# Storing a finished row tile one step later: a GpSimd-issued DMA in a two-layer attention and feed-forward kernel

## The chip, the cores and the metric

The kernel runs on one core of a Trainium2 chip. The time is that of the device in microseconds (us), of one launch. A core has the engines PE (TensorE, matmuls; PEld are its weight loads), DVE (VectorE), ACT (ScalarE), POOL (GpSimd) and SP (SyncE). In this kernel DMAs are issued from SP's queue and from POOL's queue, and run on the core's 16 DMA engines.

## The reference

All arrays are float32. `x` has 2 sequences of 2048 rows of 1024.

```python
x = x + attention(layernorm(x))        # one head: Wqkv to 3 x 256, softmax, Wo back to 1024
n = layernorm(x)
h      = relu(n @ up_w) ** 2           # 1024 -> 2048
shared = h @ down_w                    # 2048 -> 1024
lat    = (n @ fc1_w) @ expert_w        # 1024 -> 512 -> 512
routed = (lat * top2_sum(n @ gate_w)) @ fc2_w      # 512 -> 1024
x = x + layernorm(shared + routed) * ln_gamma + ln_beta
```

The change lies at the end of the last line: the layer norm of a finished tile, and its store to the result.

## The kernel before, in words

Each float32 operand is split into a high part, which ACT casts, and a low part, which DVE makes by a subtraction; a product is then three matmuls (line 130: high by high, low by high, high by low). All 4096 rows are handled in 8 row blocks of 512, and a row block in 4 row tiles of 128.

The attention comes first and is not touched by the change. Then comes the feed-forward part, a loop over `b` = 0 to 3. One `b` takes two row blocks (r = 0 and 1) together, so that a scheme of seven products (`p1` to `p7`) stands in for the eight block products of a two by two split. A `b` has two stages:

- The **up stage** runs over 70 chunks, `m` = 0 to 69, one weight piece each, 12 matmuls per chunk (`pu`).
- The **down stage** runs over the products in the order p1, p2, p6, p5, p3, p7, p4 (`j` = 0 to 6), 10 chunks each (`k` = 0 to 9), also 12 matmuls per chunk (`pd`). The rows of the first block (r = 0) are complete after p3, those of the second (r = 1) after p4. The results lie in 4 buffers `y` of the pool `unit` (14 buffers for `y`, `h`, `xh`, `xl` and `res`), two row tiles in each.

The weight pieces go round a ring of 7 buffers `w`. `stage` (L786) issues a load on SP's queue: either a raw piece `w<-wt` (L798), or one that was already split, `w<-w_p` (L795). A raw piece is cast by ACT (L815), its low half made by DVE (L823), and in b=0 for every other piece, in b=1 for every raw piece, the split piece is written back to memory from POOL's queue (`w_p<-w`, L826) to be loaded again later. The left operands of the down stage, `sp`, are cast by ACT (L1052) and finished by DVE (L1057).

A finished tile of `y` then goes through the steps of the class `Out`. `out_step` keeps a list of tiles for each step, and a call moves each tile one step further:

1. the residual row is loaded from `x1` on SP's queue (L960);
2. `add_beta`: the row vector beta is added to it by an accumulating DMA on POOL's queue (L963), and `first`: ACT sums y (L259);
3. `second`: ACT sums the squares (L271, L272);
4. `write`: DVE makes the reciprocal and two passes over y (L276, L976, L977), and POOL's queue issues the store (L978).

`out_step` is called every second chunk: in the up stage at odd `m` below 15 (tiles of r = 1 of the `b` before), in the down stage at even `k` of p7 and at k = 0 and 2 of p4 (tiles of r = 0). The last four tiles of the program take a path of their own (`late`), tile by tile behind the last matmuls.

The order is written by hand: the part lies under `tc.manual_schedule()`, so each engine and each queue runs its instructions in the order in which the program issues them, and waits at the head of its queue until that instruction's inputs are there.

Of the kernel before, what the change touches and what calls it, by code (L numbers as in the profile page):

```python
# [25 lines left out]
def kernel(  # L26
# [923 lines left out]
    class Out:  # L950
# [22 lines left out]
        def write(self):  # L973
            y, rs = self.y, self.m.inverse()
            stt = nc.vector.scalar_tensor_tensor
            stt(y, y, self.m.nm, gamma_sb, ALU.add, ALU.mult)  # L976
            stt(y, y, rs, self.res, ALU.mult, ALU.add)  # L977
            nc.gpsimd.dma_start(out=of[ds(self.n * W + self.t * P, P), :], in_=y)  # L978

    res_pair, todo, loaded, first, second = [], [], [], [], []

    def out_step():

        if second:
            second.pop(0).write()
        if first:
            second.append(first.pop(0))
            second[-1].second()  # L990
        if loaded:
            first.append(loaded.pop(0))
            first[-1].add_beta()
            first[-1].first()
        if todo:
            loaded.append(Out(*todo.pop(0)))
# [11 lines left out]
    with tc.manual_schedule():  # L1008
        for b in range(NBB):
# [70 lines left out]
            for m, (p, i) in enumerate(UP):  # L1080
                flush()
                w = next_piece()
                if p != "p2":
                    acc[i] = Pass3(acc_bank("pu"), NCC // 2)
                ps = acc[i].ps
                if p == "p2":
                    acc[i].more()
                for c in range(NCC // 2):
                    acc[i].add(piece(w, c, P, slice(0, P)), piece(X[p], c, W, slice(0, W)))
                lat, pair = i >= HU // P, i % 2 and i < HU // P  # L1090
                c22, c21 = h_at("22", i), h_at("21", i) if m >= 2 * NK else None
                if p == "p1":
                    nc.scalar.copy(c22, ps)
                elif p == "p2":
                    if lat:
                        add(h_at("11", i), ps, rwb[0], ALU.mult)
                    else:
                        relu(h_at("11", i), ps)
                        if pair:
                            square(h_at("11", i, 2))  # L1100
                elif p == "p4":
                    nc.scalar.copy(c21, ps)
                elif p == "p6":
                    add(c22, ps, c22, ALU.subtract)
                    add(c21, c21, c22, ALU.subtract)
                elif p == "p5":
                    add(c22, c22, ps, ALU.add)
                elif p == "p3":
                    c12 = h_at("12", i)
                    add(c12, c22, ps, ALU.add)  # L1110
                    if lat:
                        add(c12, c12, rwb[0], ALU.mult)
                    elif pair:
                        relu(h_at("12", i, 2), h_at("12", i, 2))
                        square(h_at("12", i, 2))
                else:
                    add(c21, c21, ps, ALU.add)
                    add(c22, c22, ps, ALU.subtract)
                    if lat:
                        add(c21, c21, rwb[1], ALU.mult)  # L1120
                        add(c22, c22, rwb[1], ALU.mult)
                    elif pair:
                        for v in ("21", "22"):
                            relu(h_at(v, i, 2), h_at(v, i, 2))
                            square(h_at(v, i, 2))

                if m % 2 and m < 15:
                    out_step()
                if b == 0 and m in (0, 1, 2, 4, 6, 8, 9, 10, 11, 12, 13):
                    norm2.step()  # L1130

                m4 = 12 if b == 0 else 10
                if m == m4:
                    x_t[1] = norm2.x
                    X["p4"] = new_x()
                if m > m4 and (m - m4) % 2 and (m - m4) // 2 < NB:
                    split_x(x_t[1], 1, (m - m4) // 2, X["p4"], split_late)
                elif m >= 2 * NK and p != "p7":
                    n = {"p4": "p6", "p6": "p5", "p5": "p3", "p3": "p7"}[p]
                    if i == 1:  # L1140
                        X[n] = new_x()
                    if i % 2 and i < 2 * NB:
                        if p == "p4":
                            sums_x(x_t, i // 2)
                        r_, f_ = PLACE[n]
                        split_x(x_t[r_], f_, i // 2, X[n], split_late)

                if m == 0:
                    ga = half("ga")[: 2 * NE, :]
                    nc.scalar.copy(ga, gate_part(X["p1"], 0))  # L1150
                elif m == 2:
                    gs = half("gs")[: 2 * NE, :]
                    add(gs, ga, gate_part(X["p2"], 1), ALU.add)
                    gt = Gate(gs)
                elif (p, i) == ("p4", 1):
                    add(ga, ga, gate_part(X["p4"], 1), ALU.add)
                elif (p, i) == ("p7", 0):
                    add(ga, ga, gate_part(X["p7"], 0), ALU.subtract)
                    gt = Gate(ga)
                if m == 6 or (p, i) == ("p7", 3):  # L1160
                    gt.largest()
                elif m == 10 or (p, i) == ("p7", 6):
                    rwb[p == "p7"] = gt.spread()
                if p == "p7" and i >= NK - 5:
                    step_s()
# [16 lines left out]
            for j, p in enumerate(("p1", "p2", "p6", "p5", "p3", "p7", "p4")):  # L1182
# [12 lines left out]
                for k in range(NK - late):  # L1195
                    flush()
                    w, s = next_piece(), next_s()
                    for t in range(NB):
                        down(t, s, w)
                    if more:  # L1200

                        if j < 6 and k < NK - 2:
                            (norm1, norm2)[j // 3].half_step()
                        if j >= 5 and k % 2 and k < 2 * NB:
                            n = "p1" if j == 5 else "p2"
                            if k == 1:
                                X[n] = new_x()
                            split_x(norm1.x, j - 5, k // 2, X[n], split_late)
                    if not more and j == 2 and k == 0:
                        ended(1)  # L1210
                        tiles = todo[-NB:]
                        del todo[-NB:]
                    elif not more and j == 3 and k % 2 == 0 and k < 2 * NB:
                        tiles[k // 2] = Out(*tiles[k // 2], row("res"))
                    elif not more and j == 4 and k % 2 == 0 and k < 2 * LATE:
                        load_early(k // 2)
                        if k < 2 * NB:
                            tiles[k // 2].add_beta()
                    if j == 5 and k % 2 == 0 or j == 6 and k in (0, 2):
                        out_step()  # L1220
                if late:
                    last_w = [next_piece() for _ in range(late)]
# [5 lines left out]
                for t in range(NB):  # L1228
                    for s, w in last if late else ():
                        down(t, s, w)  # L1230
                    ps, u, v = accs[t].ps, y_at(1, 0, t), y_at(1, 1, t)
                    if p == "p1":
                        nc.scalar.copy(u, ps)
                    elif p == "p2":
                        nc.scalar.copy(y_at(0, 0, t), ps)
                    elif p == "p6":
                        add(u, ps, u, ALU.subtract)
                    elif p == "p5":
                        add(v, u, ps, ALU.add)
                    elif p == "p3":  # L1240
                        add(y_at(0, 1, t), u, ps, ALU.add)
                    elif p == "p7":
                        add(v, v, ps, ALU.subtract)
                    else:
                        add(u, ps, u, ALU.subtract)
                    if late:
                        tiles[t].first()
                        tiles[t].second()
                        if t:
                            tiles[t - 1].write()  # L1250
                if late:
                    tiles[-1].write()
                if p == "p3":
                    ended(0)
                elif p == "p4" and not late:
                    ended(1)
            if more:
                t1 = norm1.x
        while todo or loaded or first or second:
            out_step()  # L1260


# [41 lines left out]
```

## Time and profile before

| | |
|---|---|
| median of 3 runs | 2384.47 us (2383.08 to 2388.02) |
| the profiled execution | 2384.76 us, of which the span is 2382.9 |
| granted TensorE clock | 0.995 |
| PE busy | 2335.8 us, 98% |
| DVE, ACT, POOL busy | 61%, 47%, 13% |
| DMA | 603.99 MB, mean 253 GB/s over the span |
| stores of y (L978) | 32, of 512 KB, 539 ns of POOL each, 7.2 us to landing (2.8 to 13.0) |
| beta adds (L963) | 32, of 512 KB, 10.7 us to landing |
| write-backs (L826) | 140, of 512 KB, 4.8 us to landing |
| POOL waits at L978 for y | 182.8 us in all |
| DVE waits at L977 for beta | 22.1 us in all, 15 times |

A row of a timeline reads: start, duration, engine, line, operation, output and input, count, and in brackets how long the engine was idle ahead of it and what ended that. A row of waits reads: engine, line, what it waited for, and the sum, the number and the longest of those waits. The span is what the profiler sees of one execution; the time beside it holds 1.9 us more around it. "Landing" is the time from the issue of a DMA to the arrival of its data.

### The profile page before, as it was taken

The numbers are of one execution on the slowest core, as the hardware profiler recorded it, in microseconds if no ns is written. First come the engines' busy times: TensorE is split into PE (matmuls) and PEld (weight loads), VectorE is DVE, ScalarE is ACT, GpSimd is POOL, SyncE is SP. The second block draws the span as 40 slices with busy tenths as digits, with TensorE's granted clock in tenths as the row PEclk, the third lists the DMA queues.
The fourth block names the chain that finished last, engine by engine and source line by source line (L and its number), as shares of the span: only waits on it lengthen the run. The fifth ranks groups of instructions, "written<-read, shape, count | busy, mean of one in ns | idle before, by whom it ended". The sixth has DMA issues, their size and how long they took to land.

```text
span 2382.9 us, 29281 instructions
## 1 busy us (share of the span) xinstructions
PE 2335.8 (98%) x10704; PEld 1921.8 (81%) x10704; DVE 1461.4 (61%) x2168; ACT 1131.4 (47%) x1846; POOL 298.1 (13%) x450
## 2 busy tenths in 40 slices
PE   8999999999998999999999999999999999999998
PEld 7888878888886778788778888878888877888886
DVE  5566459888877466697746467644446563445545
ACT  6555455555444543676552374644145454214224
POOL 3222111012110010011210011210000010000001
PEclk9999999999999999999999999999999999999999
DMA  5977884999996666787997789997557798655695
GB/s 196 318 257 269 278 204 127 298 315 319 290 239 181 219 228 185 228 271 259 336 309 241 237 283 333 319 342 241 193 194 262 264 330 283 208 192 184 202 312 191
DMA packets 225807, 603.99 MB, mean 253 GB/s; under 512 B 18768, under 2 KB 80720, under 8 KB 223616
## 3 DMA queue, kind: packets, MB, share of 16 engines
q1 hardware_dynamic: 152160, 334.02, 41.2%
q0 software_dynamic: 73504, 268.11, 36.8%
q8 instruction: 85, 1.39, 0.2%
q14 instruction: 58, 0.48, 0.1%
HBM read 448.96 MB, written 210.76 MB: 277 GB/s over the span
## 4 chain that ended last, share of the span: by engine, by line
PE 88%; issue 5%; DMA 4%; DVE 1%; ACT 1%; POOL 1%; SPq 0%; POOLq 0%; DVEq 0%; ACTq 0%
PE pu L130 29%; PE pd L130 26%; PE ps L130 7%; PE pq L130 7%; PE po L130 7%; PE pv L130 4%; PE pw L130 3%; DMA w<-wt 1%; PE pg L872 1%; PE pf L130 1%; DMA xt<-xt_d 1%; DMA w<-w_p 1%; PE psum L619 1%; DMA res<-in_L_ffn_ln_beta_dram 0%; DMA ew<-in_L_ffn_expert_w_dram 0%
## 5 line engine op out<-in xcount | busy, mean ns | idle before, releaser
L130 PE MATMUL pd<-w,sp 128*128 128x512 f32 x3336 | 762.5, 390 | 11.0 <-DVE sp L1057 5.6
L130 PEld LDWEIGHTS pd<-w,sp 128*128 128x128 f32 x3336 | 626.5, 188 | 145.8 <-DVE sp L1057 8.4
L130 PE MATMUL pu<-xh,w 128*128 128x512 f32 x2240 | 694.4, 391 | 7.2 <-ACT w L815 5.1
L130 PEld LDWEIGHTS pu<-xh,w 128*128 128x128 f32 x2240 | 419.6, 188 | 99.0 <-ACT w L815 6.1
L130 PE MATMUL pu<-xl,w 128*128 128x512 f32 x1120 | 436.2, 389 | 0.0
L130 PEld LDWEIGHTS pu<-xl,w 128*128 128x128 f32 x1120 | 210.4, 188 | 44.1 <-DVE xl L150 0.4
L1052 ACT CAST sp<-h 128x512 fp32r<-128x512 f32 x238 | 145.9, 618 | 193.1 <-PE pd L130 160.7
L1057 DVE TENSOR_TENSOR sp<-h,sp 128x512 fp32r<-128x512 f32 x238 | 162.4, 687 | 100.9 <-ACT sp L1052 100.6
L815 ACT CAST w<-w 128x512 fp32r<-128x512 f32 x210 | 128.3, 617 | 178.4 <-DMA w<-wt 144.7
L130 PE MATMUL po<-p,v 128*128 128x512 f32 x768 | 197.0, 395 | 2.6 <-ACT p L142 2.4
L823 DVE TENSOR_TENSOR w<-w 128x512 fp32r<-128x512 f32 x210 | 143.1, 686 | 91.3 <-ACT w L815 84.8
L130 PE MATMUL ps<-q,k 128*128 128x512 f32 x768 | 195.9, 393 | 1.8 <-DVE max L562 1.8
L130 PEld LDWEIGHTS ps<-q,k 128*128 128x128 f32 x768 | 142.4, 188 | 36.1 <-DVE max L562 6.8
L130 PEld LDWEIGHTS po<-p,v 128*128 128x128 f32 x768 | 144.1, 190 | 33.6 <-ACT p L142 3.2
L1002 ACT ACTIVATE h<-h 128x1024 f32<-128x1024 f32 x48 | 50.7, 1055 | 208.7 <-DVE h L1110 159.7
L826 POOL DMA_DIRECT2D w_p<-w x140 | 75.1, 537 | 583.1 <-DVE w L823 532.3
L150 DVE TENSOR_TENSOR xl<-xt,xh 128x512 fp32r<-128x512 f32 x104 | 71.6, 688 | 122.8 <-ACT xh L149 120.8
L557 ACT COPY s<-ps 128x512 f32<-128x512 f32 x128 | 74.8, 585 | 148.2 <-PE ps L130 147.7
L213 DVE STREAM_TRANSPOSE xblk<-xrow 128x1024 f32<-128x1024 f32 x60 | 121.1, 2019 | 9.6 <-ACT xrow L283 9.6
L562 DVE TENSOR_TENSOR max<-ps,max 128x512 f32<-128x512 f32 x120 | 82.3, 685 | 44.4 <-ACT s L557 44.1
L130 PE MATMUL pq<-xha,w_h 128*128 128x512 f32 x256 | 99.7, 389 | 0.0
L130 PE MATMUL pq<-xha,w_l 128*128 128x512 f32 x256 | 99.7, 389 | 0.0
(181 smaller groups left out, 3034.3 us busy)
## 6 DMA issues: line engine op xcount, KB each, us to landing
w<-w_p SPq DMA_DIRECT2D x350, 512.0 KB, 4.2
w_p<-w POOLq DMA_DIRECT2D x140, 512.0 KB, 4.8
w<-wt SPq DMA_DIRECT2D x210, 256.0 KB, 3.7
xt_d<-xblk POOLq DMA_DIRECT2D x56, 512.0 KB, 4.6
xt<-xt_d POOLq DMA_DIRECT2D x56, 512.0 KB, 6.6
wt<-in_L_ffn_up_w_dram POOLq DMA_DIRECT2D x9, 2048.0 KB, 25.1
wt<-in_L_ffn_down_w_dram POOLq DMA_DIRECT2D x9, 2048.0 KB, 32.3
xres<-in_L_attn_x_dram SPq DMA_DIRECT2D x32, 512.0 KB, 13.0
```

The source lines that it names most:

```text
L130: nc.tensor.matmul(self.ps, lhsT=a, rhs=b, start=self.i == 0, stop=self.i == self.n - 1, skip_group_check=self.on,)
L150: late_ops.append(lambda: nc.vector.tensor_tensor(lo, t, f32(hi), ALU.subtract))
L213: nc.vector.transpose(b.rearrange("p (q k i) -> p q k i", q=P // SQ, i=SQ), r.rearrange("p (k i q) -> p q k i", k=NCC, i=SQ),)
L557: nc.scalar.copy(s["s"][k // 4][:, ts(k % 4, W)], pm)
L562: nc.vector.tensor_tensor(s["max"], pm, s["max"], ALU.max)
L619: nc.tensor.matmul(pt[:, t : t + 1], lhsT=s["sum"][:, ds(i * W + t * P, P)], rhs=ones, start=i == 0, stop=i == 1,)
L815: nc.scalar.copy(w[:, 0:W], f32(w)[:, W : 2 * W])
L823: nc.vector.tensor_tensor(w[:, W : 2 * W], v[:, W : 2 * W], v[:, 0:W], ALU.subtract)
L826: nc.gpsimd.dma_start(out=kept[key], in_=w.bitcast(FP))
L1002: nc.scalar.activation(o, v, AF.Relu)
L1052: nc.scalar.copy(t[:, 0:W], v)
L1057: add(t[:, W : 2 * W], v, f32(t)[:, 0:W], ALU.subtract)
```

## The change

The store becomes a step of its own, `store`, behind `write`. `out_step` first stores the tile that the call before has written, then goes on as before. Since a tile now takes one call more, `out_step` is called once more in each stage: at m = 15 of the up stage and at k = 4 of p4. In the last four tiles the store follows directly on the write, as before.

```diff
             stt(y, y, self.m.nm, gamma_sb, ALU.add, ALU.mult)
             stt(y, y, rs, self.res, ALU.mult, ALU.add)
+
+        def store(self):
+            y = self.y
             nc.gpsimd.dma_start(out=of[ds(self.n * W + self.t * P, P), :], in_=y)
...
-    res_pair, todo, loaded, first, second = [], [], [], [], []
+    res_pair, todo, loaded, first, second, written = [], [], [], [], [], []
 
     def out_step():
 
+        if written:
+            written.pop(0).store()
         if second:
-            second.pop(0).write()
+            written.append(second.pop(0))
+            written[-1].write()
         if first:
             second.append(first.pop(0))
             second[-1].second()
...
-                if m % 2 and m < 15:
+                if m % 2 and m < 17:
                     out_step()
...
-                    if j == 5 and k % 2 == 0 or j == 6 and k in (0, 2):
+                    if j == 5 and k % 2 == 0 or j == 6 and k in (0, 2, 4):
                         out_step()
...
                         if t:
                             tiles[t - 1].write()
+                            tiles[t - 1].store()
                 if late:
                     tiles[-1].write()
+                    tiles[-1].store()
...
-        while todo or loaded or first or second:
+        while todo or loaded or first or second or written:
             out_step()
```

So the order in POOL's queue changes. Where the program had (b=1, p7) the store of tile 0, the beta add of tile 2, a write-back, the store of tile 1, the beta add of tile 3, it now has the beta add of tile 2, a write-back, the store of tile 0, the beta add of tile 3, a write-back, the store of tile 1. The order on the other engines and on SP's queue is the same.

## The prediction

> **What bounds the kernel now.** I read the page's totals first, then the table of windows over the stages that contain the change, then the waits of PE and of the DMA queues in those stages, and last the timeline of the worst one. The totals say that TensorE decides:
>
> ```profile
> PE 2335.8 (98%) x10704; PEld 1921.8 (81%) x10704; DVE 1461.4 (61%) x2168; ACT 1131.4 (47%) x1846; POOL 298.1 (13%) x450
> ```
>
> Whatever the change does, it can win only idle time of PE and lose only by making more of it. The windows (stretch, length, busy time of PE, PEld, DVE, ACT and POOL, granted clock, DMA share, GB/s) show where PE idles among the stages that run `out_step`:
>
> ```profile
> 1113.00:1189.00 76.00, 71.99 (x314) 58.30 (x313) 58.39 (x88) 47.79 (x92) 17.35 (x28) 1.00 0.97 324
> 1189.00:1535.00 346.00, 346.00 (x1534) 282.77 (x1533) 209.00 (x331) 172.91 (x293) 50.23 (x87) 1.00 0.85 286
> 1535.00:1590.00 55.00, 49.95 (x214) 39.07 (x213) 31.72 (x46) 22.87 (x47) 8.46 (x14) 1.00 1.02 354
> 1900.00:1985.00 85.00, 83.03 (x360) 67.58 (x359) 47.78 (x68) 39.93 (x76) 11.88 (x17) 0.98 0.92 315
> 1985.00:2359.00 374.00, 374.00 (x1657) 306.68 (x1656) 173.71 (x269) 125.11 (x204) 14.01 (x19) 1.00 0.70 230
> ```
>
> The first, third and fourth are the ends of the down stages (p7, then p4) of blocks b=0, 1 and 2: PE idles 76.00-71.99 = 4.01, 55.00-49.95 = 5.05 and 85.00-83.03 = 1.97 us. The up stages behind them and the last block up to 2359 us have none. So everything that the change can win is 4.0+5.0+2.0 = 11.0 us, 0.46% of the span. In each of the three the DMA engines are at 0.92 to 1.02 of their time. In b=1 PE is held back piece by piece (first the waits of PE from 1535 to 1590 us, then one of SP's queue from 1505 to 1590: sum, times, longest):
>
> ```profile
> PE pd L130 <- DVE sp L1057: 3.3, 4, 1.5
> PE pd L130 <- ACT junk L271: 1.7, 1, 1.7
> ```
>
> ```profile
> SPq L795 <- DMA w_p<-w: 37.9, 10, 9.1
> ```
>
> The reader should see the ring: SP may load a weight piece only when the slot's earlier piece has been written back (`w_p<-w` landed); ACT casts what lands, DVE makes the low half, PE multiplies, POOL writes back. The timeline of b=1 shows POOL's queue and DVE in it:
>
> ```profile
> 1545.16 0.54 POOL L978 DMA_DIRECT2D out_dram<-y  x1 [8.57 <-DVE y L977]
> 1546.05 0.87 POOL L963 DMA_DIRECT2D res<-in_L_ffn_ln_beta_dram  x1 [0.35 <-issue]
> 1547.78 0.55 POOL L826 DMA_DIRECT2D w_p<-w  x1 [0.86 <-DVE w L823]
> 1555.26 0.54 POOL L978 DMA_DIRECT2D out_dram<-y  x1 [6.92 <-DVE y L977]
> 1555.79 0.91 POOL L963 DMA_DIRECT2D res<-in_L_ffn_ln_beta_dram  x1
> 1561.86 1.29 DVE L977 SCALAR_TENSOR_TENSOR y<-y,rs,res 128x1024 f32<-128x1024 f32 x1 [1.20 <-DMA res<-in_L_ffn_ln_beta_dram]
> 1563.07 0.69 DVE L823 TENSOR_TENSOR w<-w 128x512 fp32r<-128x512 f32 x1
> 1564.41 5.74 PE L130 MATMUL pd<-w,sp 128*128 128x512 f32 x24 [1.50 <-DVE sp L1057]
> 1567.80 1.29 DVE L977 SCALAR_TENSOR_TENSOR y<-y,rs,res 128x1024 f32<-128x1024 f32 x1 [0.98 <-DMA res<-in_L_ffn_ln_beta_dram]
> ```
>
> The store of tile 0 stands in POOL for y (8.57 us), and the beta add of tile 2 stands behind it: it goes out at 1546.05, and tile 2's last DVE operation waits 1.20 us for it at 1561.86. Behind that on DVE are the low halves of w and of sp, and PE waits 1.50 us for the latter.
>
> **The change part by part.** It adds and removes no operation: 32 stores of 512 KB before and after, 539 ns of POOL each, and the order of instructions on PE, DVE, ACT and SP is the same. The two new calls of `out_step` (up chunk 15, p4 chunk 4) find only a store to do. The last four tiles keep their order. For the other 28, the store now stands behind the beta add that followed it, where there is one, and in b=0 and 1 mostly behind a write-back too.
>
> *The wait that goes.* Waits of POOL for y sum to 182.8 us over 32 stores, but POOL is busy 13%, so they cost nothing themselves. What counts is what stood behind them. Write-backs did not suffer: at 1547.78 one goes out 0.30 us after its DVE operation (1546.79+0.69), at 1569.99 0.29 us after, and in b=0 (1155.45 after 1154.24+0.68) 0.53 us, about POOL's own issue; I take 0. Beta adds did: those of tiles 2 and 3 go out 4 to 7 us earlier (tile 2 then waits only for its residual row, tile 3 no longer for y of tile 1). The DVE waits for tiles 2 and 3 then vanish: b=1 1.20+0.98, b=0 0.79 (tile 3). Those of tiles 0 and 1 (2.91 us at 1543.58, 1.34 in b=0) stay, because no store stood ahead of them. Of these waits PE loses what ends in its own stalls: 1.20 of the 1.50 us at 1564.41, the whole 0.20 us at 1570.35 (behind the 0.98), and 0.61 us at 1173.09 (behind the 0.79). Sum: 1.20+0.20+0.61 = 2.0 us gained. The limits: 0, if the weight piece behind each is late anyway, and the 11.0 us of all stalls. In b=2 DVE waits 2.37 and 1.97 us for these betas, but PE's only stall there is a weight load issued at 1936.38 that takes 18 us, so I take 0 of it (limits 0 and 1.97).
>
> *The traffic.* A beta add is 512 KB, which at the 354 GB/s of the b=1 window is 1.5 us of the DMA engines. Two in b=0 and two in b=1 come earlier, and about one store of each block leaves the stretch in which PE stalls. Here a rule speaks against the change. The stretch 1520 to 1590 us reads
>
> ```profile
> GB/s 321 288 379 417 380 406 424 393 367 272 234 265 373 426 369 281 307 397 419 419 327 262 368 408 320 260 389 415 404 391 316 383 287 339 417 426 419 353 323 375
> q0 software_dynamic: 3407, 12.37, 52.5%
> q1 hardware_dynamic: 4109, 12.64, 49.0%
> ```
>
> POOL's queue (q0) and SP's (q1) move equal bytes. If only the bytes counted, a store put off beyond the last stall would free 1.5 us in each of two blocks, 3.0 us in all. The Trainium skill, "DMA: Bandwidth & Descriptors", section "Queues, rings and completion order", says that each DMA engine takes turns between the queues that have work. By it SP's loads get their half for as long as POOL's queue holds anything, and betas brought forward keep it full: 0 from a later store. I take 0, since 12.37 against 12.64 MB is what turns would give, and keep -3.0 in the range. The other end is that each of the four early betas delays a weight transfer by its full 1.5 us: +6.0. The same page's "Specifications" give 358 GB/s from HBM as the limit of one core; at 354 the stalls would be pure bandwidth and no order could win anything. Slices of up to 426 GB/s in this same stretch say that it isn't a hard limit here, so I keep the 2.0.
>
> *The later release of y.* A chunk lasts 2.72 us (the spacing of SP's loads at 1520.08 and 1522.80). The last store of a first-half tile is now at p4 chunk 4, and the buffers of the tiles are claimed again from up chunk 2: 8 chunks, 21.8 us. Of a second-half tile it is up chunk 15, claimed six chunks on: 16.3 us. Stores land in 7.2 us, at most 13.0. Cover remains, so 0; if it were gone it would cost the excess of the landing over 16.3 us, and 13.0 is the longest seen. SP's order is unchanged and its loads wait for no store.
>
> Sum: -2.0 us. The profiled execution took 2384.76 us (its span 2382.9 and 1.9 around it), 0.3 above the median of 2384.47, so the difference is put on the median: 2382.5.
>
> **The rivals.** A measurement of this kernel tells about 0.2%, 4.8 us, from no change; the runs before spread over 4.9.
>
> *The ring loosens.* With the betas out of the way and the stores behind the write-backs in POOL's queue, each write-back lands sooner (it took 6.1 us from 1547.78, 7.6 from 1556.35), SP's 37.9+27.6 us of waiting in b=1 and b=0 shrink, and with them most stalls of both blocks: two thirds of 4.0+5.0, and 1 of b=2, is -7.0 us: 2377.5. For it: the ring is what PE waits for. Against: the first stalls (1548.14, 1552.44) come from transfers sent before the first store, and the DMA engines are full.
>
> *Early betas take the weights' place.* In b=1 the beta of tile 2 would go out near 1541 us, ahead of the write-back of 1547.78 and while the loads of 1533.68 and 1539.12 take 12 and 15 us to land. If all four early betas go on that path at 1.5 us each, and they then land no earlier for DVE, the time is 2384.5+5.9 = 2390.4. It decides when the write-back behind such a beta lands over 1.5 us later than the 6 to 7.6 us of now. Against: the loads' delay is already made by transfers sent before 1537.
>
> *Nothing moves.* [...]in b=2 and 3 no write-back lies between, and a store behind a beta that is ready goes out when y is done, as before. If the betas of b=0 and 1 were not what PE waits for, the time stays at 2384.5.
>
> **How the numbers follow.** The 2.0 us gain 0.40; nothing moves 0.10; the ring loosens 0.30; early betas 0.20. The first two are within 0.2%, hence faster 0.30, same 0.50, slower 0.20. Range: 7.0 of the gain side with 1 us of spread, 2376.5, up to the early betas' 2390.0; beyond lie the last part of each side, about 1 in 10.
>
> **What would show it.** POOL's store of tile 0 in b=1 should have no wait for y, and the beta of tile 2 stand before it, near 1541. DVE's waits for tiles 2 and 3 there should be gone, and the PE stalls of 1.50 and 0.20 with them; the wait of tile 0 (2.9) stays. Idle PE should read about 3.4 us in b=0, 3.6 in b=1 and 2.0 in b=2. It is wrong if SP waits longer for write-backs, if PE idles in the up stages, or if the stalls of 1548 and 1552 change by over 1 us.

## The result, and the profile after

The changed kernel takes 2380.59 us (median, 2375.90 to 2385.87) beside 2383.78 us (2380.53 to 2389.92) of the kernel before, measured side by side on one chip. The ratio is 0.9984, 95% interval 0.9976 to 0.9991: 3.8 us faster (2.1 to 5.7). That is less than the 4.8 us that the prediction called measurable, but the interval, from 17 runs of each kernel, leaves out 1. (The ratios here are those on record with their intervals; the quotient of the two medians can differ from them by some 0.0006.)

The totals of the profile after:

```profile
PE 2334.7 (98%) x10704; PEld 1922.3 (81%) x10704; DVE 1461.0 (61%) x2168; ACT 1131.2 (48%) x1846; POOL 298.3 (13%) x450
```

The work on every engine is what it was; its span is 2379.0 us, 3.9 less. So the time came out of gaps on PE, and the windows by stage say which (columns as in the prediction):

```profile
1113.00:1189.00 76.00, 72.66 (x317) 58.97 (x316) 58.35 (x88) 49.77 (x94) 17.33 (x28) 1.00 0.97 329
1189.00:1535.00 346.00, 346.00 (x1533) 282.73 (x1532) 209.31 (x332) 171.88 (x292) 49.89 (x87) 1.00 0.83 286
1535.00:1590.00 55.00, 51.60 (x223) 40.40 (x222) 32.38 (x47) 24.02 (x48) 9.03 (x16) 1.00 1.02 364
1900.00:1985.00 85.00, 83.97 (x370) 68.41 (x370) 46.95 (x68) 39.74 (x76) 11.83 (x17) 1.00 0.94 321
```

Length minus the first number behind it is PE's idle time: 3.34, 3.40 and 1.03 us in b=0, 1 and 2, where before it was 4.01, 5.05 and 1.97. That is 3.26 us less. The granted clock of the fourth row is 1.00 (0.98 before), worth another 1.6 us (last section). Up to 1113 us PE was busy 0.9 us less than before in the same length, which is not the change's doing: the first load of an `out_step` goes out only at 1126.7 us. 3.26+1.6-0.9 = 3.96 stands beside the 3.9 us between the two spans. The up stages still show no idle time (of the last, 1985 to 2359 us, PE is busy all 374).

Waits of the whole program after (engine, line, what for: sum, times, longest; L981 is now the store):

```profile
POOL out_dram L981 <- DVE y L977: 88.0, 18, 15.5
DVE y L977 <- DMA res<-in_L_ffn_ln_beta_dram: 7.9, 6, 2.7
```

POOL's wait for y is halved, which by itself is worth nothing. The second row is the one that PE can feel: it was 22.1 us in 15 waits before. Of the 14.2 us that are gone, though, 6.7 lay in the up stages, where PE doesn't idle, and 3.2 in b=2; b=0 and b=1 gave 1.3 (2.1 to 0.8) and 3.0 (5.1 to 2.1). The timeline of b=1 shows where those went:

```profile
1543.63 1.28 DVE L977 SCALAR_TENSOR_TENSOR y<-y,rs,res 128x1024 f32<-128x1024 f32 x1 [1.89 <-DMA res<-in_L_ffn_ln_beta_dram]
1545.08 0.87 POOL L963 DMA_DIRECT2D res<-in_L_ffn_ln_beta_dram  x1 [7.92 <-DMA res<-x]
1548.12 0.55 POOL L826 DMA_DIRECT2D w_p<-w  x1 [2.17 <-DVE w L823]
1548.65 0.54 POOL L981 DMA_DIRECT2D out_dram<-y  x1
...
1553.26 0.88 POOL L963 DMA_DIRECT2D res<-in_L_ffn_ln_beta_dram  x1 [4.07 <-DMA res<-x]
...
1561.08 1.28 DVE L977 SCALAR_TENSOR_TENSOR y<-y,rs,res 128x1024 f32<-128x1024 f32 x1
```

The order is the announced one: beta add of tile 2, a write-back, the store of tile 0 with no wait of its own. The last DVE operation of tile 2 (1561.08) has no bracket: its beta is there. But the beta adds are only 1.0 and 2.5 us earlier on the clock (1545.08 and 1553.26, before 1546.05 and 1555.79). What holds them now is their residual row (`res<-x`, 7.92 and 4.07 us), a wait that the store had covered. PE in the same stage, first the last stall of before, then all those of the change:

```profile
1570.35 16.41 PE L130 MATMUL pd<-w,sp 128*128 128x512 f32 x71 [0.20 <-DVE sp L1057]
```

```profile
1552.78 2.79 PE L130 MATMUL pd<-w,sp 128*128 128x512 f32 x11 [1.28 <-DVE sp L1064]
1557.31 5.94 PE L130 MATMUL pd<-w,sp 128*128 128x512 f32 x25 [1.75 <-ACT junk L271]
1563.62 22.14 PE L130 MATMUL pd<-w,sp 128*128 128x512 f32 x95 [0.37 <-DVE sp L1064]
```

The stalls of 1.28 and 1.75 are those of before (1.29, 1.66). The 1.50 and 0.20 behind the two beta waits have become one of 0.37.

### The profile page after: what moved, and what is told of

The parts are those of the page before. It is cut to its first block, busy times and chain, and to the rows that moved or that the text cites. A ratio compares the mean times of both kernels' runs of the same rounds, so it can differ in the third digit from the quotient of the medians.

```text
span 2379.0 us, 29276 instructions
## 1 busy us (share of the span) xinstructions
PE 2334.7 (98%) x10704; PEld 1922.3 (81%) x10704; DVE 1461.0 (61%) x2168; ACT 1131.2 (48%) x1846; POOL 298.3 (13%) x450
## 3 DMA queue, kind: packets, MB, share of 16 engines
q0 software_dynamic: 73504, 268.11, 37.0%
## 4 chain that ended last, share of the span: by engine, by line
PE 91%; DMA 3%; issue 2%; ACT 2%; DVE 1%; POOL 0%; SPq 0%; POOLq 0%; DVEq 0%; ACTq 0%
PE pu L130 30%; PE pd L130 28%; PE po L130 7%; PE ps L130 7%; PE pq L130 7%; PE pv L130 4%; PE pw L130 4%; DMA w<-wt 2%; PE pg L872 1%; PE pf L130 1%; DMA w<-w_p 1%; PE psum L619 1%; DMA res<-x 0%; DVE w L823 0%; DMA xt<-xt_d 0%
```

## The experiments

Three explanations were to be told apart. The first is the prediction's: **the beta add no longer stands behind a store that waits for y**, so DVE and then PE wait less. The second is the rival that **the ring of weight pieces loosens** (SP waits less for write-backs). The third is that **the store's traffic** leaves the crowded stretch. The table gathers the runs: ratio to the kernel before on the same chip, five rounds each (5 executions of e2, e10, e12 and e13, 12 to 22 of the others); the ratio times 2383 us; and PE's idle time in the three stages, from the windows of one profile each.

| kernel | ratio (95%) | us against before | PE idle b=0, 1, 2 | sum |
|---|---|---|---|---|
| before | | | 4.01, 5.05, 1.97 | 11.0 |
| the change | 0.9984 (0.9976 to 0.9991) | -3.8 | 3.34, 3.40, 1.03 | 7.8 |
| e1_beta_first | 0.9987 (0.9978 to 0.9997) | -3.1 | 3.66, 3.95, 1.10 | 8.7 |
| e2_beta_behind | 1.0032 (1.0019 to 1.0044) | +7.6 | 6.64, 6.93, 1.80 | 15.4 |
| e3_up_only | 0.9998 (0.9990 to 1.0006) | -0.5 | 3.60, 5.10, 0.60 | 9.3 |
| e4_two_steps | 0.9983 (0.9974 to 0.9991) | -4.1 | 4.75, 3.12, 0.53 | 8.4 |
| e5_no_beta | 0.9981 (0.9973 to 0.9989) | -4.5 | 2.49, 1.85, 0 | 4.3 |
| e6_no_store | 0.9991 (0.9983 to 0.9999) | -2.1 | 3.13, 3.19, 0 | 6.3 |
| e8_late_start | 0.9995 (0.9987 to 1.0003) | -1.2 | 3.01, 5.69, 0 | 8.7 |
| e9_res_early | 0.9981 (0.9975 to 0.9987) | -4.5 | 3.48, 2.59, 0 | 6.1 |
| e11_early_not_put_off | 0.9984 (0.9978 to 0.9991) | -3.8 | 3.43, 3.54, 0 | 7.0 |
| e12_rows_in_p3 | 0.9963 (0.9950 to 0.9975) | -8.8 | 2.42, 2.00, 0 | 4.4 |
| e13_p3_not_put_off | 0.9966 (0.9952 to 0.9979) | -8.1 | 1.80, 1.63, 0 | 3.4 |
| e10_res_in_p3 | 0.9950 (0.9936 to 0.9963) | -11.9 | 1.65, 0.82, 0 | 2.5 |

What one profile's sum saves against the 11.0 of before and what the ratio says differ by up to 3.4 us, so a sum alone does not rank two kernels that lie close. The profile of e9 is that of its slowest execution (2384.42 us, its median is 2377.69). Part of what it lost lies ahead of the three stages: up to 1113 us PE was busy 1085.1 us, with the change 1087.6.

**e1_beta_first.** The wait in POOL's queue is taken from the beta add in another way: the store stays where it was before the change, and the beta add goes out ahead of it. No call of `out_step` is added.

```diff
     def out_step():
+        if loaded:
+            loaded[0].add_beta()
         if second:
             second.pop(0).write()          # with the store in it, as before
...
             first.append(loaded.pop(0))
-            first[-1].add_beta()
```

> The store stays where it was, directly behind y's last operation and ahead of the write-back; only the beta add of the same call is put ahead of it. Theory A (the gain is the beta adds that no longer stand behind a store): the whole gain is here, -3 us against the kernel before (0.9987), idle PE in the three stages near 3.3 + 3.4 + 1.0 = 7.7 us, no wait of DVE for the betas of tiles 2 and 3 of b=1. Theory B (the gain is the store that no longer stands ahead of a write-back): 0 us, idle PE near the 11.0 us of before.

0.9987, and the change's ratio lies in its interval. The stores still wait for y (5.82 us for the one at 1564.06), and that costs nothing. Its interval leaves out 1. So a gain of this size comes without the store put off, as soon as the beta add is out from behind it.

**e2_beta_behind.** The reverse: the change, but with the beta adds of tiles 2 and 3 one call later, behind the store of the tile two ahead.

```diff
             second.append(first.pop(0))
+            if second[-1].t > 1:
+                second[-1].add_beta()
             second[-1].second()
...
-            first[-1].add_beta()
+            if first[-1].t < 2:
+                first[-1].add_beta()
```

> The store is put off a step as in the change, but the beta adds of tiles 2 and 3 are put off too and stand behind it, so they leave at about the time of the kernel before. Theory A: gain gone, 0 us (0.9990 to 1.0010), the DVE waits for beta at tiles 2 and 3 of 1 us or more and the PE stall of about 1.5 us at the third wait of b=1 back. Theory B: the gain stays, -3 us, and SP's waits for write-backs in b=1 are shorter than the 37.9 us of before.

1.0032: 7.6 us slower than before, where the expectation was a return to before. The beta adds of tiles 2 and 3 leave later than before, not at about the same time: at 1550.74 and 1559.08 (before 1546.05 and 1555.79; this stage as a whole runs some 1.9 us later). What stands ahead of them now is the store with a write-back ahead of it, which waits for DVE. The timeline of its b=1 shows the beta add behind the store, the DVE operation that waits for it, and the write-back behind that:

```profile
1558.36 0.53 POOL L981 DMA_DIRECT2D out_dram<-y  x1
...
1559.08 0.88 POOL L963 DMA_DIRECT2D res<-in_L_ffn_ln_beta_dram  x1 [0.19 <-issue]
...
1566.56 1.29 DVE L977 SCALAR_TENSOR_TENSOR y<-y,rs,res 128x1024 f32<-128x1024 f32 x1 [4.00 <-DMA res<-in_L_ffn_ln_beta_dram]
...
1568.74 0.55 POOL L826 DMA_DIRECT2D w_p<-w  x1 [8.78 <-DVE w L823]
```

and PE's row there the stall that follows:

```profile
1569.10 21.15 PE L130 MATMUL pd<-w,sp 128*128 128x512 f32 x85 [4.36 <-DVE sp L1067]
```

The late beta stops DVE for 4.00 us at 1562.56; the low halves of w and sp come late, and PE stands for 4.36. ACT had cast that weight piece at 1560.64, so the piece was not what was missing. From the late beta on, this is the prediction's chain, made larger; that a store waiting for y is what delays the beta, e2 doesn't test. It also speaks against the ring as the cause: SP's waits for write-backs in 1500 to 1590 us are shorter here than in the change,

```profile
SPq L795 <- DMA w_p<-w: 27.2, 8, 7.2
```

27.2 against 35.8 us (37.9 before), and yet PE idles 3.5 us more in that stage. In e1, which is faster than before, they are longer than before:

```profile
SPq L795 <- DMA w_p<-w: 40.2, 9, 9.1
```

And they are longest in the three fastest kernels below (40.9 us in e10, 43.3 in e12, 47.6 in e13) and shortest in e5 (10.3), which is about as fast as the change. So waiting less in SP's queue is not what makes a kernel faster here.

**e3_up_only.** Only the stores of the second row blocks (r = 1), which run in the up stage, are put off.

```diff
-            written.append(second.pop(0))
-            written[-1].write()
+            o = second.pop(0)
+            o.write()
+            if o.n % 2:
+                written.append(o)
+            else:
+                o.store()
```

> Only the stores of the second-half tiles, which fall into the up stage, are put off; those of the first-half tiles (p7 and p4) stay as in the kernel before. Both theories: PE never idles in the up stages, so 0 us (0.9992 to 1.0008), idle PE 11 us in the three down stages, 0 in the up stages. A third theory, that the up stage gains or loses (buffers of y released later), would show PE idle there.

0.9998 (0.9990 to 1.0006), PE idle 5.10 us in b=1. The up stages neither win nor lose anything that shows; what the change wins, it wins in p7 and p4 (the two intervals touch only at 0.9990 to 0.9991). In b=2 this kernel idles 0.60 us though its down stages have the order of before, where it was 1.97: the difference of 1.97 and 1.03 in b=2 can't be put down to the change.

**e4_two_steps.** In the down stages the store is put off by one call more (k = 6 of p4 is added).

```diff
-            written.append(second.pop(0))
-            written[-1].write()
+            o = second.pop(0)
+            o.write()
+            written.append([2 if o.n in (0, 2, 4) else 1, o])   # calls left
...
-                    if ... or j == 6 and k in (0, 2, 4):
+                    if ... or j == 6 and k in (0, 2, 4, 6):
```

> The stores of first-half tiles of b=0, 1 and 2 are put off by two steps, so that two of them, not one, leave the stretch in which PE stalls. Theory A: the betas leave as in the change, so it is as fast as the change, -3 us against the kernel before, idle PE 7.7 us. Theory B and the count of bytes (1.5 us for each 512 KB that leaves the stretch): 1 to 3 us more than the change, -4 to -6 us, idle PE 5 to 6.5 us.

0.9983: as the change. With the beta add ahead, one step more for the store made no difference that could be resolved.

**e6_no_store, e5_no_beta.** The traffic, taken away: the 12 stores, or the 12 beta adds, of the down stages are left out.

```diff
# e6_no_store
-            written.pop(0).store()
+            o = written.pop(0)
+            if o.n not in (0, 2, 4):
+                o.store()
# e5_no_beta
-            first[-1].add_beta()
+            if first[-1].n not in (0, 2, 4):
+                first[-1].add_beta()
```

> The changed kernel without the stores of the first-half tiles of b=0, 1 and 2, so 12 of the 32; those rows of the output are not written. Theory A and the rule that queues take turns: nothing waits for these stores, about as fast as the change, -3 us against the kernel before, idle PE 7 to 8 us. Traffic theory: 1.5 us for each store that still falls before the last stall, two in b=0 and two in b=1: -6 to -9 us, idle PE 2 to 5 us.

> The changed kernel without the beta adds of the first-half tiles of b=0, 1 and 2, so 12 of the 32; the output lacks beta there. It takes away both the wait of DVE and 12 transfers of 512 KB. Theory A (what is left to win lies in waiting for betas): against the changed kernel only the DVE waits of tile 0 (0.8, 1.9, 0.7 us) and of b=2 go, 1 to 2 us, -5 us against the kernel before, idle PE about 6.5 us. Traffic theory (every 512 KB taken out of the full stretches saves 1.5 us): four in each block, up to all idle time of b=0 and 1: idle PE 1 to 3 us, -9 us.

Without the stores 0.9991, no faster than with them: even by the opposite ends of the two intervals all 12 stores are worth at most 1.9 us, where counting bytes promised 2 to 5 us more than the change. So the third explanation falls. Without the beta adds 0.9981: 0.7 us below the change, at most 4.3 by the opposite ends of the intervals, and not distinguishable from it. The rows of POOL's queue in the pages (packets, MB, and the packets' time as a share of 16 engines' span) of the change, e5 and e6 give the size of one:

```profile
q0 software_dynamic: 73504, 268.11, 37.0%
```

```profile
q0 software_dynamic: 71776, 261.81, 35.7%
```

```profile
q0 software_dynamic: 71776, 261.81, 36.3%
```

37.0% of 2379.0 less 35.7% of 2375.1 is 32.3 us for 12 beta adds: 2.7 us each. For the 12 stores (36.3% of 2376.1) it is 17.7 us, 1.5 each. The same 73504 packets took between 36.8 and 37.1% in the twelve profiles that have them, or some 7 us between the extremes, so both figures are good to about 0.5 us.

**e8_late_start.** The steps of a tile in the down stages of b=0 to 2 start two calls later, at k = 4 of p7, when its rows have been complete for longer, and end correspondingly later.

```diff
-  if j == 5 and k % 2 == 0 or j == 6 and k in (0, 2, 4):
+  if (j == 5 and k % 2 == 0 and (k > 2 or not more)
+          or j == 6 and k % 2 == 0 and (k < 6 or more)):
```

> The changed kernel with the whole chain of steps of the first-half tiles (residual load, beta, statistics, write, store) begun two calls later in b=0, 1 and 2, at p7 chunk 4, away from the three fetches of x tiles that POOL issues in the first chunks of p7. Theory A: the betas land sooner once they no longer share with these fetches, DVE's wait for tile 0 goes, and stalls of the first weight loads (ACT's waits of 7 and 3 us in b=1) shrink: idle PE 3 to 6 us, -5 to -8 us. Theory of full DMA engines: the same bytes in the same stage, stalls only move: idle PE 7 to 9 us, -2 to -4 us. If buffers of y come free too late for the up stage, PE idles there and it is slower than the change.

0.9995 (0.9987 to 1.0003), less than either theory expected, and PE idles 5.69 us in b=1, though no DVE operation waits for a beta in that stage. The timeline shows what PE lacks instead:

```profile
1550.93 0.62 ACT L815 CAST w<-w 128x512 fp32r<-128x512 f32 x1 [4.71 <-DMA w<-wt]
...
1553.57 10.27 PE L130 MATMUL pd<-w,sp 128*128 128x512 f32 x37 [3.14 <-ACT junk L271]
```

ACT waits for raw weight pieces to land (8.67 us for the one that it casts at 1542.76, then the 4.71 above; 7.32 and 3.27 with the change), and PE stops at 1550.43, half a microsecond before the second has landed. PE goes on 2.64 us after that cast begins. The stall of 1.75 us that the change left alone reads the same way: a cast at 1554.66 behind a wait of 3.27 us, and PE 2.65 us later. So the beta waits are one of two things that PE idles for in this stage; the other is the landing of raw weights, which this kernel makes worse.

**e9_res_early.** The change left the beta adds waiting for their residual rows. Here the first call in p7 loads two rows, so tiles 1 to 3 have theirs one call earlier.

```diff
-        if todo:
-            loaded.append(Out(*todo.pop(0)))
+        for _ in range(2 if todo and todo[0][:2] in ((0, 0), (2, 0), (4, 0)) else 1):
+            if todo:
+                loaded.append(Out(*todo.pop(0)))
```

> The changed kernel with the residual rows of tiles 1 to 3 loaded one call earlier in b=0, 1 and 2, so that POOL's beta adds find them landed (the change's POOL waits of 7.9 and 4.1 us for them in b=1 and of 8.8 and 8.4 in b=2). Theory A carried on: the betas of tiles 2 and 3 leave 4 to 8 us earlier once more; but DVE no longer waits for those in b=0 and 1, so only b=2 can gain, 0 to 1 us: -3 to -5 us against the kernel before. Rival (early transfers take the weights' place): idle PE of b=1 1 to 2 us more than the 3.4 of the change, -1 to -2 us.

0.9981, overlapping with the change; PE idle in b=1 is 2.59 us. No POOL wait for a residual row is left in b=1, but DVE still waits 6.9 us for beta over the program (7.9 with the change), 4.8 of it in b=2. Earlier rows alone, inside the same stretch, bring nothing that could be resolved.

**e10_res_in_p3.** So the residual rows move out of the stretch: they are loaded in the last part of p3 (k = 4, 6 and 8; in b=1 at 1501.42 to 1512.30 us, before at 1520.45 to 1536.78), where the rows of r = 0 are not complete yet but their residuals are known, and the beta adds follow from k = 8 of p3 on.

```diff
+    pre, hold = [], []
...
-        if loaded:
+        if pre:
+            pre.pop(0).add_beta()
+        if loaded and hold:
+            hold.pop()
+        elif loaded:
             first.append(loaded.pop(0))
-            first[-1].add_beta()
+            if first[-1].n not in (0, 2, 4):
+                first[-1].add_beta()
...
+                    if more and j == 4 and k in (4, 6, 8):
+                        for t in {4: (0, 1), 6: (2,), 8: (3,)}[k]:
+                            o = Out(2 * b, t, y[t // 2][:, ts(t % 2, C)])
+                            loaded.append(o)
+                            pre.append(o)
+                        if k == 8:
+                            pre.pop(0).add_beta()
+                            hold.append(1)
...
-                if p == "p3":
+                if p == "p3" and not more:
                     ended(0)
```

> The changed kernel with residual rows and beta adds of the first-half tiles of b=0, 1 and 2 one to two calls earlier than in e9: the rows are loaded in the last chunks of p3, the betas leave from the last chunk of p3 to p7 chunk 4; statistics, writes and stores stay where they are in the change. Theory A: no DVE wait for beta is left in these stages (e9 still has 2.1 us in b=1 and 4.8 in b=2), idle PE 4 to 5.5 us (e9: 3.5 + 2.6 + 0), 0 to 1.5 us below e9, so -5 to -6.5 us against the kernel before, 0.9973 to 0.9979. Rival (bytes moved into p3 only shift the full stretch): PE stalls appear in p3 of b=1, as fast as e9 or slower, -3 to -5 us.

0.9950 (0.9936 to 0.9963), the fastest of all (medians 2372.78 and 2383.21 us, whose quotient is 0.9956), and about twice the gain that was expected. Its windows:

```profile
1113.00:1189.00 76.00, 74.35 (x326) 60.68 (x325) 59.67 (x89) 48.03 (x92) 17.36 (x28) 1.00 0.98 336
...
1535.00:1590.00 55.00, 54.18 (x236) 42.33 (x235) 32.35 (x47) 26.16 (x52) 8.39 (x14) 1.00 1.00 367
...
1900.00:1985.00 85.00, 85.00 (x376) 68.81 (x375) 42.79 (x61) 34.94 (x66) 11.67 (x16) 1.00 0.95 326
```

Idle PE is 1.65, 0.82 and 0 us, while the DMA engines are as full as before (1.00 of their time in b=1, 367 GB/s). No DVE operation of the program waits for a beta. In b=1 PE has two stalls left:

```profile
1550.72 5.96 PE L130 MATMUL pd<-w,sp 128*128 128x512 f32 x25 [0.53 <-issue]
1556.85 22.25 PE L130 MATMUL pd<-w,sp 128*128 128x512 f32 x95 [0.17 <-DVE sp L1070]
```

The stall of 1.28 us, which the change left alone, is gone too, and that of 1.75 (ahead of the same 25 matmuls) is down to 0.53. It moves every byte of the change and is faster than e5, which leaves 12 transfers out. So here it counts more when the transfers run than how many bytes they are.

**e12_rows_in_p3, e13_p3_not_put_off, e11_early_not_put_off.** These take e10 and e9 apart. e12 is e10 with the residual rows early, but the beta adds at the change's calls (no `pre`). e13 and e11 are e10 and e9 with the store directly behind `write` and the beta add ahead of both:

```diff
-        if written:
-            written.pop(0).store()
+        if pre:                        # e11: if loaded: loaded[0].add_beta()
+            pre.pop(0).add_beta()
         if second:
-            written.append(second.pop(0))
-            written[-1].write()
+            o = second.pop(0)
+            o.write()
+            o.store()
```

> e10 with only the residual rows loaded in p3; the beta adds leave at the calls of the changed kernel (p7 chunks 2 to 8), but never wait for a row. Theory A (what counts is when the betas leave): between e9 and e10, since betas leave as in e9: about -5 us against the kernel before, 0.9981. Theory of the crowded stretch (what counts is that four row loads no longer fall between the weight loads of p7): near e10, -9 to -12 us.

> e10 without the change itself: every store directly behind its tile's last operation, as in the kernel before; rows and betas of the first-half tiles early as in e10. Theory A: no beta add stands behind a store any more, so the change is worth nothing here: as fast as e10, -10 to -12 us, 0.9950. If the store's place behind the write-back is worth something of its own, it is 1 to 3 us slower than e10.

> e9 without the change itself: residual rows a call earlier, the beta add ahead of the store in the call, and the store of every tile directly behind its last operation, ahead of the write-back. Theory A: betas leave as in e9, so as fast as e9, -4.8 us against the kernel before (0.9975 to 0.9987). If the store's own place behind the write-back is worth something, it loses that against e9: about -3 us.

e12 reaches 0.9963: most of e10's gain comes with the earlier rows alone, though its beta adds go out at 1529.46 to 1545.06 in b=1 and DVE still waits for some (7.7 us in the program, 7.9 with the change). In the stretch 1500 to 1590 us ACT waits 19.0 us for raw weights in e12 and 15.8 in e10, against 23.6 in the change. That fits residual rows no longer delaying the landing of weights, but no run alters that delay alone, so this mechanism is argued, not shown. Whether early beta adds bring more (0.9950 against 0.9963) stays open, since the intervals overlap.

e13 (0.9966) against e10, e11 (0.9984) against e9, and e1 against the change are three pairs that differ in whether the store is put off. In each the one put off is ahead, by 0.0016, 0.0003 and 0.0003; every pair's intervals overlap (and two of the pairs were run on different chips, each against the kernel before on its own). So the store's own place was resolved in none. e13 has no DVE wait for beta in the three stages either, and is 8.1 us faster than before without the change.

## Why the prediction was right, point by point

- **The mechanism** held: e1 wins about the same without delaying a store, by the beta add alone, and e2, with the store delayed and the beta late, loses 7.6 us. The prediction's own limit, that the weight piece behind the wait might be late anyway, did not come in: in the kernel before ACT cast that piece at 1559.00, and DVE came to it only at 1563.07.
- **The size** was -2.0 us, and -3.8 (-5.7 to -2.1) was measured. In b=0 and 1 the terms fit, with 0.67+1.65 = 2.3 us less idle time in all: idle PE read 3.34 and 3.40 us for "about 3.4" and "3.6". The stall of 0.61 in b=0 is gone, and 1.50+0.20 in b=1 shrank by 1.33 for a predicted 1.40; a further 0.30 went at 1548, which was not expected. A remainder of DVE's wait for tile 3, 0.21 us, stayed. The two terms that were missing lie in b=2, which the prediction took at 0: the stall fell from 1.97 to 1.03, and the clock drop behind it, 1.6 us, is not in the profile after. Neither can be assigned to the change, since e3's down stages have the order of before and its idle time there is 0.60. So of the measured 3.8 us some 2.3 are accounted for, near the lower end of the interval, and whether the rest is the change's is open.
- **"Beta adds go out 4 to 7 us earlier"** failed. Tile 2's left at 1545.08 instead of near 1541. The step had freed POOL's queue but not the residual row, which landed 7.92 us after POOL was ready. On the clock it was 1 us earlier, and that this was about enough for a wait of 1.20 us is luck: the gain came out as forecast though the beta add did not leave when it was forecast to.
- **The wait of tile 0** was to stay at 2.9 and read 1.89 us. Nothing that the change moves lies ahead of it in the stage, and it reads 3.06, 2.58 and 2.00 us in e1, e3 and e4, so this is the scatter of one stage of one profile, and about as large as the gain of a whole stage.
- **The traffic of later stores, 0**, with -3.0 in the range: e6 confirms the 0, and counting bytes would have been wrong. The rule of turns that the prediction took from the Trainium skill ("DMA: Bandwidth & Descriptors", section "Queues, rings and completion order") had said 0 too, but no run here tests it. Its turns go by whole packets, of which the two queues had 3407 and 4109 in that stretch, and their nearly equal bytes are no more than what the program issues on each.
- **The early betas, 0 with +6.0** as the other end: right, but the price of 1.5 us was a store's. A beta add takes 2.7 us of the DMA engines by e5 against the change. The rival that they take the weights' place fell with e9 and e10, which send them still earlier and are not slower. The upper end of the range, 2390.0, lay a little below this rival's own 2390.4.
- **"The ring loosens"**: SP's waits for write-backs did shrink, in b=1 from 37.9 to 35.8 and in b=0 from 27.6 to 21.1 us, and the time alone hardly tells the two apart: 2380.59 lies 1.9 us from the forecast and 3.1 from this rival's 2377.5. But e2 has shorter waits in b=1 still and is slower, and e1, e10, e12 and e13 have longer ones than before and are faster, so they are not the cause.
- **The later release of y, 0**: e3 and e4 agree, and their up stages show no idle PE.

## What to carry to other kernels

A DMA that waits for its input at the head of a queue need not cost anything by its own wait (in e1 the stores still wait 115.1 us in all, and e1 keeps the gain); ask what is queued behind it and who waits for that, and move that ahead (e1) rather than measure the wait. When such a wait goes, look for the next input of the freed instruction: here it was the residual row, and the kernels that move that row's load out of the stretch where the DMA engines are full (e12, and e10 with the beta adds moved as well) are 8.8 and 11.9 us faster than before, two to three times the change. Where every engine's work is unchanged, look at the idle time of the bounding engine by stage and at its clock; but one profile gives them only to within a microsecond or two per stage.

## What the runs showed of the hardware that was not expected

**A short gap can cost more than its length.** The kernel before idles 1.97 us in b=2. The matmuls behind that gap, and two windows there (columns as above; the third from the end is the granted clock):

```profile
1954.64 26.37 PE L130 MATMUL pd<-w,sp 128*128 128x512 f32 x108 [1.97 <-DMA w<-w_p]
```

```profile
1956.00:1958.00 2.00, 2.00 (x7) 1.53 (x6) 2.00 (x6) 0.00 (x0) 0.56 (x1) 0.50 1.07 283
1958.00:1960.00 2.00, 2.00 (x8) 1.59 (x7) 1.25 (x2) 0.94 (x2) 0.00 (x0) 0.67 1.01 324
```

The clock is at half for some 3.4 us, from about 1956.0 on, and the 108 matmuls take 26.37 us, where the change takes 24.77 behind its gap of 1.03:

```profile
1952.71 24.77 PE L130 MATMUL pd<-w,sp 128*128 128x512 f32 x108 [1.03 <-DMA w<-w_p]
```

So that gap of 1.97 us cost 1.6 more. The same followed gaps of 2.08 us in e3 (b=0), 3.14 in e8 and 4.36 in e2 (both b=1). Summed over windows of 1 us, each of the four drops takes the same 1.7 us of clock, half speed for 3.4 us, however long the gap was. But none followed 2.55 us in e2 (b=0), 2.42 in e3 (b=1), 1.96 in e4 or any shorter gap of the three stages. So no length decides alone. The Trainium skill, "TensorE: Matmul & The Clock Gate", section "Part 1: The HAM clock gate (the "warmup" mystery)", has the half clock after at least one idle window of about 3.4 us, in windows that run free of the program. Free-running windows would fit the scatter, and a drop of 3.4 us would be one window long, but no trace shows the windows; and gaps of 1.97 and 2.08 us are shorter than the idle window given. There the measurement decides.

**An accumulating DMA is dearer than a plain one.** By the queue rows above, 512 KB added to a tile took 2.7 us of the 16 engines' packet time and 512 KB stored 1.5 us, each good to about 0.5 us. Even so, leaving 12 of the former out won nothing that could be resolved over the change.
